# A decoder layer on one core: the first mask loaded with the weights, and a halved clock after longer stops in the account that orders TensorE

## The chip, the core and the metric

The kernel runs on one core of one Trainium2 chip. The metric is the device time of one execution in microseconds (us), as the median of several runs. A profile of one further execution shows what each engine did: TensorE (PE for its matmuls, PEld for its weight loads), VectorE (DVE), ScalarE (ACT), GpSimd (POOL) and SyncE (SP), which issues nearly all the DMA transfers.

## The reference, cut to what matters

The input x has 4 batches of 1024 rows of 256 values. One decoder layer is computed in float32, with 16 heads of 16 values each:

```python
x = x + self_attention(layernorm(x))      # causal, scores from two mixed products, biases
x = x + cross_attention(layernorm(x), ctx_1024, mask)   # 77 context rows
x = x + ffn(layernorm(x))                 # silu(x Wg') * (x Wu'), then Wd'; hidden size 768
```

In the cross attention, places where the mask is true get the score -1e9 before the softmax:

```python
scores = jnp.where(masked[:, None, :, :], NEG, scores)
```

The mask comes as 4 x 1024 x 77 booleans, one byte each. A batch's mask is 77 KB.

## The kernel before, in words

**Chunks and parts.** Each batch is cut into two chunks of 512 rows, so there are eight chunks. For each chunk the same parts are computed. `project` normalises the rows, transposes them (`L182`) and multiplies them with the key, query and value weights (`L755`, `L813`). `maxima` computes the scores once (`L853`, the causal mask added by `L861`) only to take each row's maximum on VectorE (`L866`); after every second group of heads the maxima are transposed (`L736`) and turned into a matmul operand (`L740`). `attend` computes the scores again, transposed (`L936`), subtracts the maxima with one more matmul (`L942`), takes the exponential on ScalarE (`L955`) and weighs the values (`L979`); `L668` transposes the result back and `L706` is the output product. `cross_attention` does the same against the 77 context rows (`L755` with `xwq`, maxima `L1097` and `L1105` with VectorE's `L1111`, scores `L1151`, `L1164`). `ffn` has matmuls into the hidden layer (`L1220`) and out of it (`L1254`), with ScalarE, VectorE and GpSimd in between (`L1226` to `L1231`).

**Spread tiles.** Keys and queries have to lie on other partitions than the product leaves them on. `spread` (`L713`) writes each product as two halves, hi on ScalarE (`L718`) and lo on VectorE (`L721`), and eight DMA transfers per product on SP's queue (`L727`) copy them to their places: 128 KB each, 1 MB per product.

**Start.** All weights and the rows of the first two chunks (x00, x01) are requested in the first 9 us on the queues of SP and ACT. VectorE and TensorE are ordered by hand there, until a flag "begun" is set in `maxima`; from then on TensorE alone is. The stream `late_weights` runs once "begun" is set: it builds `sel` and `selB` (`selections`, `L512` to `L524`), requests the first batch's mask (`load_mask(0)`, `L532`, its transfer is `L1015`), clears some tiles on GpSimd (`L533` to `L536`), and prepares the cross attention's weights. It ends in `load_cross(0)`, which reads the mask on VectorE: `L1038` reduces it to one value per row (`keep`), `L1040` turns it into `mneg`. `load_ffn` fetches the feed-forward weights as integers (`wi`, `L628`), GpSimd converts them (`L630`), VectorE reduces their largest value into `big` (`L632`) and TensorE transposes them (`L644`).

**What sets the order of the work.** Each part is a Python generator that yields pieces. A piece tells its TensorE time, the work that follows it on other engines, and the buffers that it takes. `weave` holds an account of the chip: the end of TensorE's last piece, the busy spans of ACT, DVE, POOL and DMA, and the time at which each buffer comes free. Again and again it computes when each stream's next piece could start, adds that stream's entry of `LATES` for the chunk, and issues the piece that could start first. So every duration in the account bears on the order of all the later pieces. There are three `pair` buffers and two `single` buffers in PSUM; a piece of `maxima` takes a `pair`, which comes free when VectorE has reduced it. TensorE executes the pieces in exactly the order written. VectorE, ScalarE, GpSimd and SP's queue also work through fixed orders of their own, so an instruction that waits there holds back what stands behind it.

The account so far let TensorE run at one speed:

```python
s.end = t + p["pe"]
if p["pe"]:
    tensor.update(end=s.end, mode=p["mode"])
```

Of the kernel before, what the change touches and what calls it, by code (L numbers as in the profile page):

```python
# [19 lines left out]
P = 128  # L20
# [7 lines left out]
def tile_decoder_layer(  # L28
# [110 lines left out]
    def x_rows(b, n):  # L139
        xt = wide([P, QT, D], "xr")  # L140
        nc.sync.dma_start(xt, x[b, n * CH : (n + 1) * CH, :].rearrange("(t p) d -> p t d", p=P))
        return xt
# [44 lines left out]
    def transpose_rows(xn):  # L187
# [2 lines left out]
        nc.scalar.copy(xnT, t)  # L190
        return xnT


    stage_cm = tc.tile_pool(name="stage", bufs=1)
    stage = stage_cm.__enter__()
# [26 lines left out]
    wo_n = rows_in(Wo, NC, F32, "wo_n", nc.sync)  # L222
    nc.sync.dma_start(bo_b, bo.partition_broadcast(P))
    x01 = x_rows(0, 1)

    et = stage.tile([P, HD, MS], F32, name="et")
    nc.vector.memset(et, 0.0)
# [200 lines left out]
        def last(self):  # L428
            return max(z for _, z in self.spans)

    tensor = {"end": 0.0, "mode": None}
    busy = {k: Engine() for k in ("ACT", "DVE", "POOL", "DMA")}
    flags = set()

# [17 lines left out]
    def piece(pe, use=(), at=0.0, cond=None, free=(), mode="whole", **take):  # L452

        return dict(pe=pe, use=use, at=at, cond=cond, free=free, mode=mode, take=take)

    def weave(*streams, until=None):
        while True:
            live = [s for s in streams if s.next is not None]  # L460
            if not live or until in flags:
                return
            can = []
            for s in live:
                p = s.next
                if p["cond"] is not None and not p["cond"]():
                    continue
                t = max(
                    tensor["end"], p["at"], *(slots[k].when(c) for k, c in p["take"].items()), 0.0
                )  # L470
                if p["pe"] and p["mode"] != tensor["mode"]:
                    t += SWITCH
                if p["use"] and p["take"]:

                    eng, us = p["use"][0]
                    t = max(t, busy[eng].start(t + p["pe"], us) - p["pe"] - 1.0)
                if t < 1.0e8:
                    can.append((t + (s.lates[s.chunk] if s.lates else 0.0), t, s))
            assert can, [s.next for s in live]
            soon = min(c[0] for c in can) + WAIT  # L480
            _, t, s = next(c for c in can if c[0] <= soon)
            p = s.next
            s.got = {k: [slots[k].take() for _ in range(c)] for k, c in p["take"].items()}
            s.end = t + p["pe"]
            if p["pe"]:
                tensor.update(end=s.end, mode=p["mode"])
            for token in p["free"]:
                give(token, s.end)
            s.done = s.end
            for eng, us in p["use"]:  # L490
                s.done = busy[eng].run(s.done + LATE, us)
            s.next = next(s.pieces, None)
# [33 lines left out]
    def late_weights(st):  # L526

        yield piece(0.0, w4=1, use=[("DVE", 4.0)], cond=lambda: "begun" in flags)
        selections(wide([P, NHP, P], "sel_f"))
        st.release("w4")  # L530
        flags.add("selections")
        load_mask(0)  # L532
        nc.gpsimd.memset(mneg, 0.0)  # L533
        nc.gpsimd.memset(xpad, 0.0)
        nc.gpsimd.tensor_copy(k2s, zero.to_broadcast(k2s.shape))
        nc.gpsimd.memset(v2, 1.0)  # L536
        nc.sync.dma_start(xwo, xWo.rearrange("(n p) f -> p n f", p=P))
        yield piece(0.0, w4=3, use=[("DMA", 4.0), ("POOL", 8.0)])
        toks = st.got["w4"]
        reorder(xwq, raw_weights(xWq))  # L540
        give(toks.pop(), st.done)
        raw = raw_weights(xWk)
        xwk = wide([P, NC, D], "xwk")
        reorder(xwk, raw)
        give(toks.pop(), st.done)
        yield piece(0.0, es=2, use=[("DMA", 4.0)])
        (t_en, t_enT) = st.got["es"]
        en = weights_tile("en").rearrange("p a b -> p (a b)")
        en = en.rearrange("p (b d) -> p b d", d=D)[:S2, :B, :]
        nc.sync.dma_start(en, enc.rearrange("b s d -> s b d"))  # L550
        enT = weights_tile("enT")[:, :, :SB]
        for c in range(NC):
            yield piece(
                0.5, single=1, use=[("DVE", 0.5)], at=st.done,
                free=[t_en] if c == NC - 1 else [],
            )
            t = single()
            for b in range(B):
                nc.tensor.transpose(
                    t[:, b * S2 : (b + 1) * S2],  # L560
                    en[:, b, c * P : (c + 1) * P],
                    ident[:S2, :S2],
                )
            nc.vector.tensor_copy(enT[:, c, :], t[:, :SB])
            st.release("single")
        yield piece(0.0, es=2)
        kk = st.got["es"]
        hi = weights_tile("khi", F32R)[:, :, :SB]
        lo = weights_tile("klo", F32R)[:, :, :SB]
        for k in range(NC):  # L570
            yield piece(
                1.1, single=1, use=[("ACT", 0.4), ("DVE", 0.5)], at=st.done + 0.5,
                free=toks if k == NC - 1 else [],
            )
            t = single()
            for c in range(NC):
                nc.tensor.matmul(
                    t[:, :SB], xwk[:, c, k * P : (k + 1) * P], enT[:, c, :],
                    start=(c == 0), stop=(c == NC - 1),
                )  # L580
            nc.scalar.copy(hi[:, k, :], t[:, :SB])
            nc.vector.tensor_tensor(
                lo[:, k, :], t[:, :SB], hi[:, k, :].bitcast(F32), ALU.subtract
            )
            st.release("single")
        nc.sync.dma_start(k2_dram[0], hi.bitcast(F32))
        nc.sync.dma_start(k2_dram[1], lo.bitcast(F32))
        for k in kk:
            give(k, st.done + 3.0)
        yield piece(0.0, w4=2, use=[("DMA", 4.0)])  # L590
        toks = st.got["w4"]
        raw = raw_weights(xWv)
        v2f = wide([P, B, D], "v2f")
        ready = st.done
        for b in range(B):
            yield piece(
                0.9, single=1, use=[("ACT", 0.4)], at=ready,
                free=[toks.pop(0), t_enT] if b == B - 1 else [],
            )
            t = single()  # L600
            for c in range(NC):
                nc.tensor.matmul(
                    t[:S2, :D], enT[:, c, b * S2 : (b + 1) * S2], raw[:, c, :],
                    start=(c == 0), stop=(c == NC - 1),
                )
            nc.scalar.copy(v2f[:S2, b, :], t[:S2, :D])
            st.release("single")
        nc.sync.dma_start(v2_dram, v2f[:S2])
        give(toks[0], st.done + 3.0)
        load_cross(0)  # L610
        flags.add("cross weights")
# [157 lines left out]
    def project(st, b, n):  # L769

        if (b, n) == (0, 0):
            yield piece(0.0, w4=1)
            xnT, t_x, at = x00T, st.got["w4"], 0.0
        else:
            yield piece(
                0.0, use=[("DMA", 4.0)] * (b > 0) + NORM, w4=1,
                cond=lambda: (("half", b - 1) if b else ("projected", 0, 0, 0)) in flags,
            )
            t_xn = st.got["w4"]
            xn = x01 if (b, n) == (0, 1) else x_rows(b, n)  # L780
            normal_rows(xn, *row_scales(xn))
            yield piece(
                1.1, use=[("ACT", 1.05)], at=st.done + LATE, pair=1, w4=1, free=t_xn
            )
            xnT = transpose_rows(xn)
            st.release("pair")
            t_x = st.got["w4"]
            at = st.done + LATE
        for c in range(NC):
# [8 lines left out]
            if c == 0:  # L798
                for i in range(QT):
                    if i % 2 == 0:  # L800
                        yield piece(
                            2.0, use=[("ACT", 1.8)] if i else [],
                            **({} if i else {"pair": 1, "v": 1}),
                        )
                        if i == 0:
# [202 lines left out]
        return nat, t_nat  # L1008


    masks, mks = {}, {}

    def load_mask(b):
        mks[b] = xpool.tile([P, NT, S2], U8, tag="mk", name="mk", bufs=2)
        nc.sync.dma_start(mks[b], mask[b].rearrange("(t p) s -> p t s", p=P))  # L1015

    def load_cross(b):

# [251 lines left out]
    def every(part, lates, chunks=range(NQ)):  # L1270
# [8 lines left out]
        return Stream(pieces, lates)  # L1279

    LATES = (
        [-0.05, 0.00, 0.00, 0.00, -0.09, 0.00, -0.11, 0.02],
        [0.00, 0.00, -0.09, 0.00, 0.00, 0.00, 0.00, -0.48],
        [0.00, 0.00, 0.00, 0.00, 0.00, 0.00, 0.00, 0.00],
        [-3.63, 0.00, 0.00, 0.00],
        [0.74, 0.00, 0.00, 0.15],
        [0.00, -0.15, -0.34, 0.00, 0.00, 0.41, 0.00, 0.00],
    )
    streams = [
        every(maxima, LATES[0]), every(cross_attention, LATES[1]), every(attend, LATES[2]),  # L1290
# [67 lines left out]
```

## Time and profile before

| what | value |
|---|---|
| median of 3 runs | 1239.33 us (1238.6 to 1239.84) |
| the profiled execution's own time | 1236.36 us |
| its span, first to last instruction | 1234.6 us |
| TensorE's matmuls busy | 1108.7 us (90% of the span) |
| VectorE busy | 729.8 us (59%) |
| ScalarE busy | 561.2 us (45%) |
| GpSimd busy | 130.5 us (11%) |
| mean granted TensorE clock | 0.956 |

The table says how busy each engine was. The granted clock is the share of its full speed that TensorE was given; at 0.5 a matmul takes about twice as long. It is recorded for every stretch of the execution, and where it is below 1, a stretch can be longer without more work in it. A row of a timeline gives the start, the duration, the engine, the line, what is written from what, and in brackets the idle time ahead of it and what ended that.

### The profile page before, as it was taken

What the parts mean: (1) busy time and instruction counts of PE and PEld (TensorE: products, weight loads), DVE (VectorE), ACT (ScalarE), POOL (GpSimd) and SP (SyncE); (2) the same over time, 40 slices, a digit from 0 to 9 for tenths busy, and PEclk for the clock granted to TensorE, in tenths of its full rate; (3) what the DMA queues carried; (4) which work ended last, traced back from release to release, by engine and by line L of the source; (5) the groups of instructions that cost most, each with busy time, mean ns of one, the idle gap of its engine ahead of it and who ended that gap; (6) DMA issues with size and microseconds to landing.
All of it is one profiled execution on the core that took longest, in us unless ns stands there. A gap on an engine that the chain in (4) does not pass through costs nothing. (4 is left out here: it accounts for less than half of the span.)

```text
span 1234.6 us, 22019 instructions
## 1 busy us (share of the span) xinstructions
PE 1108.7 (90%) x9059; PEld 683.7 (55%) x9059; DVE 729.8 (59%) x1247; ACT 561.2 (45%) x801; POOL 130.5 (11%) x138
## 2 busy tenths in 40 slices
PE   6489999999789999999899899899999899897975
PEld 4355545556556457557656456556656555456664
DVE  4577686254677867245777863652667746516443
ACT  3035455644343564653343555355344364572421
POOL 3230000001200003001200000201110000002112
PEclk9689999999999999999899899899899999998987
DMA  6973425457242014566533016363823314005000
GB/s 119 162 140 79 66 43 70 69 86 99 39 72 35 6 43 71 88 86 98 71 56 52 6 26 103 56 92 57 104 37 53 48 38 49 18 1 67 19 35 19
DMA packets 65437, 76.44 MB, mean 62 GB/s; under 512 B 22450, under 2 KB 39398, under 8 KB 65331
## 3 DMA queue, kind: packets, MB, share of 16 engines
q1 hardware_dynamic: 64227, 74.62, 38.7%
q8 instruction: 73, 1.20, 0.5%
q10 hardware_dynamic: 1104, 0.35, 0.1%
q14 instruction: 33, 0.27, 0.1%
HBM read 15.28 MB, written 9.33 MB: 20 GB/s over the span
## 5 line engine op out<-in xcount | busy, mean ns | idle before, releaser
L866 DVE TENSOR_REDUCE mt<-pair 128x2 f32<-128x1024 f32 (+3 forms) x384 | 352.6, 953 | 96.0 <-PE pair L861 60.8
L955 ACT ACTIVATE es<-pair 128x1024 f32<-128x1024 f32 (+3 forms) x384 | 300.2, 811 | 227.8 <-PE pair L949 158.1
L853 PE MATMUL pair<-k,q 64*128 64x512 f32 (+3 forms) x768 | 163.8, 432 | 39.9 <-DVE mt L866 15.1
L936 PE MATMUL pair<-q,k 64*128 64x512 f32 (+3 forms) x768 | 163.7, 423 | 18.5 <-DVE mt L866 9.7
L979 PE MATMUL single<-es,vs 128*32 128x512 f32 (+3 forms) x1536 | 163.3, 498 | 0.0
L853 PEld LDWEIGHTS pair<-k,q 64*128 64x128 f32 x768 | 76.8, 192 | 122.8 <-DVE mt L866 44.5
L942 PE MATMUL pair<-ms,sel 64*128 64x512 f32 (+3 forms) x768 | 135.8, 350 | 0.0
L936 PEld LDWEIGHTS pair<-q,k 64*128 64x128 f32 x768 | 73.5, 188 | 106.8 <-issue 38.4
L1231 POOL TENSOR_TENSOR hT<-h,hT 128x512 fp32r<-128x512 f32 x48 | 61.3, 1277 | 336.3 <-ACT hT L1230 310.4
L1153 ACT ACTIVATE es<-pair 77x1024 f32<-77x1024 f32 x64 | 63.1, 1018 | 35.6 <-PE pair L1151 35.1
L942 PEld LDWEIGHTS pair<-ms,sel 64*128 64x128 f32 x768 | 74.6, 191 | 2.8
L1254 PE MATMUL pair<-wdT,hT 128*128 128x256 f32 x384 | 61.9, 311 | 14.8 <-POOL hT L1231 4.1
L861 PE MATMUL pair<-cm_qk,id 64*128 64x64 bf16 (+1 forms) x1024 | 70.2, 214 | 0.0
L1226 ACT ACTIVATE h<-pair 128x512 f32<-128x512 f32 x48 | 28.6, 597 | 88.4 <-PE pair L1220 75.0
L949 PE MATMUL pair<-cm_kq,id 64*128 64x64 bf16 (+1 forms) x1024 | 67.0, 210 | 0.0
L1254 PEld LDWEIGHTS pair<-wdT,hT 128*128 128x128 f32 x384 | 53.8, 206 | 23.8 <-POOL hT L1231 5.2
L158 POOL TENSOR_TENSOR rs<-ve,mhalf 128x4 f32<-128x4 f32 x24 | 24.3, 1011 | 389.1 <-DVE ve L156 389.0
L1111 DVE TENSOR_REDUCE mx<-pair 128x8 f32<-128x616 f32 x64 | 48.4, 793 | 28.2 <-PE pair L1105 27.8
L1227 DVE SCALAR_TENSOR_TENSOR h<-h,pair 128x512 f32<-128x512 f32 x48 | 32.9, 684 | 54.0 <-ACT h L1226 50.0
L663 ACT COPY aS<-single 128x512 f32<-128x512 f32 x64 | 37.7, 588 | 45.5 <-PE single L1164 29.8
L190 ACT COPY xnT<-pair 128x1024 f32<-128x1024 f32 x32 | 32.5, 1014 | 48.8 <-PE pair L182 48.8
L979 PEld LDWEIGHTS single<-es,vs 128*32 128x32 f32 x1536 | 32.1, 108 | 39.7 <-issue 29.4
(180 smaller groups left out, 1589.9 us busy)
## 6 DMA issues: line engine op xcount, KB each, us to landing
q<-hi SPq DMA_DIRECT2D x128, 128.0 KB, 5.0
q<-lo SPq DMA_DIRECT2D x128, 128.0 KB, 6.0
k<-hi SPq DMA_DIRECT2D x64, 128.0 KB, 4.0
k<-lo SPq DMA_DIRECT2D x64, 128.0 KB, 6.3
xr<-in_x_dram SPq DMA_DIRECT2D x8, 512.0 KB
x<-in_x_dram SPq DMA_DIRECT2D x8, 512.0 KB, 7.1
x_dram<-x SPq DMA_DIRECT2D x8, 512.0 KB, 2.6
out_dram<-x SPq DMA_DIRECT2D x8, 512.0 KB, 3.9
```

The lines of the kernel that those rows point to most:

```text
L853: nc.tensor.matmul(t[:, j, :w], q[r, a, i * P : (i + 1) * P], k[r, a, :w], start=True, stop=True,)
L861: nc.tensor.matmul(t[:, j, w - P + 64 * half : w], id2[r, half], cm_qk[r, half, 64 * half :], start=False, stop=True, skip_group_check=True,)
L866: nc.vector.tensor_reduce(mt[:, i, :, p, kc], t[:, :, :w], AX.X, ALU.max)
L936: nc.tensor.matmul(t[:, j, lo:], k[r, a, ki * P : (ki + 1) * P], q[r, a, lo:], start=True, stop=False,)
L942: nc.tensor.matmul(t[:, j, lo:], sel[r, hp, :], ms[r, lo:], start=False, stop=True)
L949: nc.tensor.matmul(t[:, j, lo : lo + 64 * (half + 1)], id2[r, half], cm_kq[r, half, : 64 * (half + 1)], start=False, stop=True, skip_group ...
L955: nc.scalar.activation(es[:, :, lo:], t[:, :, lo:], AF.Exp)
L979: nc.tensor.matmul(acc[0][W * jj : W * (jj + 1), lo:], vs[:, ki, V1 * h : V1 * h + W], both[jj // 2][:, jj % 2, lo:], start=(kb == 0), sto ...
L1111: nc.vector.tensor_reduce(mt[:, i, h4 : h4 + 4, :].rearrange("q (k p) j -> q k (p j)", k=2), tv[:, :, :, :S2], AX.X, ALU.max,)
L1153: nc.scalar.activation(es[:S2], t[:S2], AF.Exp)
L1231: nc.gpsimd.tensor_tensor(hs[:, 1, :], h, hs[:, 0, :].bitcast(F32), ALU.subtract)
L1254: nc.tensor.matmul(t[:, i, :], h[1][:, v, i * P : (i + 1) * P], w[:, h[0], :], start=(m == 0), stop=(m == len(terms) - 1),)
```

## The change

Four edits, all in the order and the account; no matmul, reduction or transfer is added or left out.

1. `load_mask` is defined earlier, and `load_mask(0)` is called with the loads of the weights, right behind the request for x01. The call in `late_weights` goes.
2. The account keeps a time `slow`. If TensorE has stood for more than `REST` (1.3 us) ahead of a piece, `slow` is set to `COLD` (5.0 us) after the piece's start; a piece that starts before `slow` is charged with half of what is left of that stretch, at most with its own length.
3. `project` sets a flag when the second chunk's rows are normalised, and the value product of the first chunk is held back until then.
4. The entries of `LATES` have new values.

```diff
@@ beside transpose_rows @@
+    mks = {}
+
+    def load_mask(b):
+        mks[b] = xpool.tile([P, NT, S2], U8, tag="mk", name="mk", bufs=2)
+        nc.sync.dma_start(mks[b], mask[b].rearrange("(t p) s -> p t s", p=P))
@@ start @@
     x01 = x_rows(0, 1)
+    load_mask(0)
@@ the account @@
-    tensor = {"end": 0.0, "mode": None}
+    tensor = {"end": 0.0, "mode": None, "slow": 0.0}
+    REST, COLD = 1.3, 5.0
@@ weave @@
             s.end = t + p["pe"]
             if p["pe"]:
+                if t - tensor["end"] > REST:
+                    tensor["slow"] = t + COLD
+                s.end += min(max(tensor["slow"] - t, 0.0) / 2, p["pe"])
                 tensor.update(end=s.end, mode=p["mode"])
@@ late_weights @@
         flags.add("selections")
-        load_mask(0)
         nc.gpsimd.memset(mneg, 0.0)
@@ project @@
             normal_rows(xn, *row_scales(xn))
+            flags.add(("normal", b, n))
...
                             2.0, use=[("ACT", 1.8)] if i else [],
+                            cond=lambda: (b, n) != (0, 0) or ("normal", 0, 1) in flags,
                             **({} if i else {"pair": 1, "v": 1}),
@@ ahead of load_cross @@
-    masks, mks = {}, {}
-
-    def load_mask(b):
-        mks[b] = xpool.tile([P, NT, S2], U8, tag="mk", name="mk", bufs=2)
-        nc.sync.dma_start(mks[b], mask[b].rearrange("(t p) s -> p t s", p=P))
+    masks = {}
@@ LATES @@
-        [-0.05, 0.00, 0.00, 0.00, -0.09, 0.00, -0.11, 0.02],
-        [0.00, 0.00, -0.09, 0.00, 0.00, 0.00, 0.00, -0.48],
+        [0.00, 0.00, 0.00, 0.00, -0.03, 0.00, -0.31, 0.00],
+        [0.00, 0.00, 0.00, 0.00, 0.00, 0.00, -0.23, 0.00],
         [0.00, 0.00, 0.00, 0.00, 0.00, 0.00, 0.00, 0.00],
-        [-3.63, 0.00, 0.00, 0.00],
-        [0.74, 0.00, 0.00, 0.15],
-        [0.00, -0.15, -0.34, 0.00, 0.00, 0.41, 0.00, 0.00],
+        [-1.02, 0.03, 0.00, -0.48],
+        [0.54, 0.47, 0.00, 0.31],
+        [-0.20, -0.15, -0.42, -0.02, 0.00, 0.33, 0.00, 0.00],
```

The rows of `LATES` belong to, in this order: maxima, cross attention, attend, the projections of a batch's first and of its second chunk, and ffn.

## The prediction

> **What bounds the kernel now.** I read the page first, then the busy time by stretches, then the longest waits in the timeline. The page says that TensorE is the bound as a whole, and where it is not:
>
> ```profile
> PE 1108.7 (90%) x9059; PEld 683.7 (55%) x9059; DVE 729.8 (59%) x1247; ACT 561.2 (45%) x801; POOL 130.5 (11%) x138
> ...
> PE   6489999999789999999899899899999899897975
> ...
> PEclk9689999999999999999899899899899999998987
> DMA  6973425457242014566533016363823314005000
> ```
>
> The reader is to see the second and third digit: in these 62 us TensorE is half idle, the clock is lowest and the DMA engines are fullest. The stretches show how the start divides:
>
> ```profile
> core 0: us, PE busy (x) PEld busy (x) DVE busy (x) ACT busy (x) POOL busy (x), PEclk, DMA share, GB/s
> 27.40:38.30 10.90, 0.00 (x0) 0.00 (x1) 6.71 (x14) 0.69 (x1) 4.71 (x6) 0.61 1.08 123
> 38.30:50.80 12.50, 10.30 (x78) 7.88 (x78) 7.44 (x15) 1.70 (x2) 0.00 (x0) 0.66 1.07 130
> 50.80:59.40 8.60, 0.04 (x2) 0.04 (x2) 2.82 (x9) 0.00 (x0) 0.59 (x1) 0.67 1.17 213
> 59.40:92.50 33.10, 29.64 (x270) 18.04 (x270) 24.27 (x33) 10.79 (x17) 12.07 (x14) 0.83 0.78 149
> 92.50:142.80 50.30, 46.68 (x487) 27.30 (x483) 36.63 (x49) 25.79 (x53) 2.06 (x3) 1.00 0.37 72
> ```
>
> There are two stops, 10.9 and 8.6 us. The first waits for the spread keys and queries (`L727`, 126 GB/s with the DMA engines full). The second has this cause:
>
> ```profile
> 49.50 0.37 SPq L1015 DMA_DIRECT2D mk<-in_mask_BxSxS_bk_dram  x1
> 56.58 0.80 DVE L1038 TENSOR_REDUCE keep<-mk 128x8 f32<-128x616 uint8 x1 [8.51 <-DMA mk<-in_mask_BxSxS_bk_dram]
> 59.36 0.58 PE L853 MATMUL pair<-k,q 64*128 64x256 f32 x2 [8.62 <-DVE mt L866]
> ```
>
> The mask is requested behind four spread products and lands 7.1 us later. VectorE stands at `L1038`; behind it stand the reductions `L866`, so the three `pair` buffers stay full and TensorE stops. After 92.5 us TensorE is busy 46.7 of 50.3 us at full clock: from there the start's gain passes on to the end.
>
> **The change part by part.** My sum is made against the profiled execution's 1236.4 us (span 1234.6). It lies 3.0 us below the median of the runs, 1239.3, so I add 3 at the end.
>
> *The mask's load.* One request of 77 KB moves behind x01's, on SP at about 9.3 us. No spread product can be asked for before 19.57 us (the first `L727`), and from 12.5 to 20 us the DMA share is 0.06, so it lands under cover. If that cover were gone it would delay the spread keys by at most its own 7.1 us; I take 0. SP's queue now has the mask's request ahead of four spread products instead of behind them. The 8.51 us of VectorE's wait go: +8.6 us at TensorE, if nothing else is late.
>
> *The clock.* After the stop TensorE ran at half speed until about 67.3 us (the half-clock stretch of 2.5 us slices ends there), so 7.7 us of its work took twice as long: 3.9 us more. The Trainium skill, "TensorE: Matmul & The Clock Gate", section "What's actually happening", says that about 3.4 us of sustained work restore the clock; that would make it 1.7 us. The first stop speaks as the trace does (work from 39.8, full clock at about 46.9 us), so I use 3.9. Together 12.5 us are at stake.
>
> *The second chunk's normalisation comes earlier.* The order of the changed program has x01's normalisation (`L153` to `L166`) ahead of the lo half of the second key product on VectorE, and its eight transposes (`L182`, 1.97 us at 44.78) and ScalarE's copy inside the first stop instead of behind the first eight maxima. That takes 1.97 and the 1.10 us wait behind it out of the stretch 38.3 to 50.8. But TensorE then puts x01's key product (3.8 us at half clock, as `L755` at 63.36) between the seventh and eighth maxima, and VectorE has its lo half (0.75 us, behind ScalarE's 0.69) between the seventh and eighth reduction. I estimate 3 us of slip there: the eighth reduction ends near 50 instead of 46.8 us.
>
> *VectorE's chain from there.* 1.3 us of selections, 0.8 of `keep`, 2.3 of the other pieces, 6.5 of eight reductions and a lo half of 0.75 put the copy `L874` near 62 instead of 68.57 us: about 7 us earlier.
>
> *What is late next.* Before, x01's second key product was spread at 115 us. In the new order its eight transfers (1 MB, 8.3 us at 126 GB/s) stand on SP ahead of `en` and the first `wi`. The DMA engines were full from 20 to 85 us, so the feed-forward weights land later:
>
> ```profile
> 81.34 1.04 POOL L630 CAST wi<-wi 128x1024 f32<-128x1024 int32 x1 [14.14 <-DMA wi<-in_L_ffn_w_gate_dram]
> 92.00 1.21 DVE L632 TENSOR_REDUCE big<-wi 128x1 f32<-128x1024 f32 x1
> ```
>
> The cast moves from 81.34 to about 88 us (8.3, less about 1.5 for the gap at 67.5 to 70 us and the mask's place), so `big` can start near 89. VectorE comes to it after 33 reductions instead of 34, at about 83 us by the sum above (62, then 16 reductions and three small ones in 21 us). It waits some 5 to 6 us, and again reductions and `pair` buffers stand behind it. Against 92.0 that leaves 3 us. TensorE does keep more: by this place it has done x01's second key product (1.9 us, before at 110.9) and about 2 us of `attend` that came later before. I take 3 + 4 = 7, less 2 for a clock that falls in this stop: **5 us** gained at the start. Its bounds are -1 us (the whole wait and a full half-clock stretch) and 12.5.
>
> *The account and LATES.* They cost no instruction; they set another order. Up to the second batch the two orders are the same for long stretches (about 140 to 285 us), and in the second, third and last batch for others; in between feed-forward pieces lie elsewhere. For the price I use the wait for a cross attention's spread queries: it takes 14.0 us from the first `xwq` product (1122.20) to the first score:
>
> ```profile
> 1122.20 1.98 PE L755 MATMUL single<-xnT,xwq 128*128 128x512 f32 x4 [0.67 <-ACT xnT L190]
> ...
> 1136.21 1.11 PE L1105 MATMUL pair<-k2s,q 128*128 128x156 f32 x4 [4.41 <-DMA q<-hi]
> ...
> 313.04 3.69 PE L1254 MATMUL pair<-wdT,hT 128*128 128x256 f32 x16 [3.40 <-DVE mt L866]
> ...
> 779.07 1.97 PE L182 MATMUL pair<-ident,xr 128*128 128x128 f32 x8 [4.13 <-DVE xr L166]
> ```
>
> Counted in the orders with the trace's spacing (0.23 us a hidden matmul, 0.12 a `L1254`), the work inside this time falls from 13.0 to 10.0 us in the third chunk, 13.1 to 10.0 in the fifth, 9.0 to 8.1 in the last: up to 7.0 us lost. Against that, the stretches in which the stops at 313 (3.40) and 779 (4.13) lie are cut up anew: up to 7.5 us gained. I take 0 and keep -10 to +10 for the range.
>
> Does the account charge rightly? The skill's page (section "What's actually happening") lets the clock fall only after an idle window of about 3.4 us, so REST = 1.3 would charge stops that cost nothing, up to 2.5 us each. The trace has both:
>
> ```profile
> 598.40 2.68 PE L1254 MATMUL pair<-wdT,hT 128*128 128x256 f32 x16 [1.89 <-ACT es L955]
> ...
> 596.00:608.00 12.00, 9.32 (x45) 6.81 (x44) 7.22 (x13) 2.77 (x5) 2.62 (x4) 0.72 0.65 87
> ...
> 1062.00:1074.00 12.00, 9.99 (x73) 6.05 (x71) 2.12 (x5) 7.27 (x10) 0.00 (x0) 1.00 0.00 1
> ```
>
> 1.89 us at 598.40 was followed by a clock of 0.72; 2.01 us at 1064.35 by 1.00. By the page the charge would misplace pieces at the short stops (201, 598, 681, 763, 984, 1064 and 1223 us), by up to 2.5 us each; by the trace it is right about half the time. I follow the trace and give it no sign.
>
> Sum: 1236.4 - 5 + 0 = 1231.4, and 3 for the median: **1234.4 us**.
>
> **The rivals.**
> *More is kept (20%).* The wait at `big` is short, because the DMA engines catch up, or the new account also shortens later stops. For it: no wait but the mask's holds VectorE longer than 5 us in the start. Against: the full DMA engines. 12.5 us, or 5 and as much later: 1225 to 1230.
> *The wait only moves (16%).* `big` waits until 92 for `wi`, or the later order takes the gain: 1239.
> *The fill of the queries' wait is gone (24%), slower.* Feed-forward pieces are issued earlier, and the third, fifth and last chunk's cross attention lack them: 7.0 us of waits, and two new stops over 3 us, each with some 3.4 us at half clock as after 313 (1.7 us lost each): 10.4 against 5 gained, 1244.8. It decides from 7.5 us on.
> That the change does not do what it says: the mask's move stands in the program's order, so only the account could fail, as weighed above; this is within the 16%.
>
> **How the numbers follow.** My forecast has 40%. A difference of 0.2%, 2.5 us, is about what a measurement of this kernel can tell from no change. Faster: 40 + 20 = 60%; same 16%; slower 24%. The range takes in the upper case and most of the slower one: 1223 to 1247; the forecast's own range is 1230 to 1237.
>
> **What would show it.** Right: `L1038` without a wait; no stop of TensorE near 50 to 59 us; the clock at 1 from about 47 us; `L632` waiting for GpSimd's cast near 83 to 89 us; the first `nat` transpose near 138 instead of 142.8 us. Wrong: that transpose near 130 or at 143; `wi` cast before 84 us; stops over 4 us at `L1105` in the third and fifth chunk would show the slower rival.

## The result, and the profile after

The changed kernel takes 1227.74 us (median of 8 runs, 1224.94 to 1234.12) against 1239.14 us (median of 8, 1235.65 to 1240.44). The ratio is 0.9917, with a 95% interval of 0.9894 to 0.9941. So it is faster, by 11.4 us in this comparison; two more comparisons of the same kernel, told below, gave 9.3 and 7.9 us. The gain lies beyond the forecast's own range (1230 to 1237), and at the place of the rival "more is kept".

The profiled execution of after has a span of 1231.1 us and a time of 1232.86 us. That is 5.1 us above the median of its runs, while the one of before lay 2.8 us below its median. So the two profiles laid side by side show only 3.5 us of the gain, and the rest has to be looked for with care. The page first:

```profile
PE 1110.8 (90%) x9059; PEld 684.9 (56%) x9059; DVE 729.9 (59%) x1247; ACT 562.6 (46%) x801; POOL 130.8 (11%) x138
...
PE   6679989999999898999898998999999889996875
...
PEclk9798999999999999999999998999999989998986
DMA  6992315537732016555533015444826140006000
```

TensorE's instructions and their sum are those of before (1110.8 against 1108.7 us). Only the places of the stops differ: the second digit of its row rises from 4 to 6. The page's third digit of the DMA row rises too, from 7 to 9. The stretches of the start show both more finely:

```profile
core 0: us, PE busy (x) PEld busy (x) DVE busy (x) ACT busy (x) POOL busy (x), PEclk, DMA share, GB/s
27.40:38.30 10.90, 4.33 (x11) 2.24 (x11) 3.04 (x4) 1.70 (x2) 1.16 (x2) 0.69 1.08 123
38.30:50.80 12.50, 10.66 (x74) 6.74 (x74) 8.82 (x18) 1.38 (x2) 0.00 (x0) 0.73 1.08 131
50.80:59.40 8.60, 6.13 (x34) 4.10 (x34) 7.04 (x15) 0.00 (x0) 0.00 (x0) 0.60 1.08 136
59.40:92.50 33.10, 26.17 (x290) 15.42 (x292) 20.68 (x30) 14.22 (x22) 10.90 (x12) 0.96 0.98 196
92.50:142.80 50.30, 47.38 (x442) 27.36 (x441) 36.18 (x46) 23.17 (x48) 3.87 (x5) 0.93 0.20 52
```

From 50.80 to 59.40 TensorE worked 0.04 us before and 6.13 us now: the second stop is gone, though two waits of 1.70 and 1.62 us and a lowered clock (0.60) are left in its place. From 59.40 to 92.50 it does less than before (26.17 against 29.64 us), with the DMA share at 0.98 instead of 0.78. The timeline of after says what happens there. Its line numbers are shifted: `L1047` was `L1038`, `L879` was `L866`, `L738` was `L727`, `L641` and `L643` were `L630` and `L632`.

```profile
50.09 0.78 DVE L1047 TENSOR_REDUCE keep<-mk 128x8 f32<-128x616 uint8 x1
...
61.18 0.18 DVE L887 COPY mpad<-mt 128x32 f32<-128x32 f32 x1
...
74.27 3.82 SPq L738 DMA_DIRECT2D k<-hi  x4
78.19 2.47 SPq L738 DMA_DIRECT2D k<-lo  x4
81.35 0.40 SPq L639 DMA_DIRECT2D wi<-in_L_ffn_w_gate_dram  x1
...
88.31 1.04 POOL L641 CAST wi<-wi 128x1024 f32<-128x1024 int32 x1 [13.03 <-DMA wi<-in_L_ffn_w_gate_dram]
89.38 1.22 DVE L643 TENSOR_REDUCE big<-wi 128x1 f32<-128x1024 f32 x1 [4.22 <-POOL wi L641]
```

`keep` (`L1047`) no longer waits. `mpad` is copied at 61.18 instead of 68.57 us. Then the second chunk's key spread (`L738`, eight transfers) stands on SP ahead of the first `wi`, which is cast at 88.31 instead of 81.34 us, and VectorE waits 4.22 us for it. Of 8.6 us taken away, 3.55 us reach the first transpose of `nat` (a chunk's attention output): 139.24 instead of 142.79 us.

In this profile the lead then shrinks to 1.5 us at 277 us. The next gain comes after 285 us. Of before and then of after:

```profile
285.00:310.00 25.00, 22.47 (x114) 16.13 (x112) 13.03 (x28) 8.97 (x16) 3.64 (x5) 1.00 0.99 126
310.00:335.00 25.00, 19.29 (x156) 14.22 (x156) 16.18 (x24) 8.79 (x13) 5.55 (x5) 0.93 0.32 43
```

```profile
285.00:310.00 25.00, 25.00 (x132) 19.90 (x130) 15.19 (x24) 9.79 (x16) 7.69 (x6) 1.00 0.69 84
310.00:335.00 25.00, 23.11 (x262) 13.91 (x260) 18.52 (x35) 12.16 (x20) 1.21 (x2) 1.00 0.77 108
```

TensorE is busy 48.1 of these 50 us instead of 41.8: the 3.40 us stop at 313 and its lowered clock are gone, and two shorter ones at 305 and 322 (1.28 and 1.16 us) with them. The two orders can be compared exactly at the places where both have done the same matmuls. Between two such places TensorE takes 154.81 us instead of 165.12 for the same work, since it is idle for 9.0 us instead of 17.3; first before, then after:

```profile
277.12:442.24 165.12, 147.86 (x1334) 91.66 (x1334) 115.34 (x165) 70.67 (x103) 13.27 (x11) 0.99 0.34 49
```

```profile
275.66:430.47 154.81, 145.85 (x1334) 89.71 (x1333) 113.64 (x164) 70.57 (x101) 12.32 (x10) 1.00 0.43 59
```

So the lead is 11.8 us at 442 us. Later much of that is given back. New or longer stops of TensorE are

```profile
480.25 0.64 PE L1114 MATMUL pair<-k2s,q 128*128 128x156 f32 x4 [2.60 <-DMA q<-lo]
...
763.01 1.11 PE L1114 MATMUL pair<-k2s,q 128*128 128x156 f32 x4 [2.94 <-issue]
...
988.59 0.79 PE L949 MATMUL pair<-q,k 64*128 64x512 f32 x2 [3.80 <-DVE mt L879]
...
1126.23 1.11 PE L1114 MATMUL pair<-k2s,q 128*128 128x156 f32 x4 [5.33 <-DMA q<-hi]
```

With the same matmuls done, the lead is 8.4 us at the third batch's rows (500.79 instead of 509.21 us), 13.0 from 704 to 742, 10.9 at 1117, 4.8 at the last transpose of `xn` (normalised rows; 1187.03 instead of 1191.78) and 3.5 at the end. The last part, with the last chunk's cross attention and `ffn`, costs 7.4 us of it. Before, then after:

```profile
1117.42:1234.60 117.18, 87.43 (x454) 64.53 (x452) 54.46 (x97) 34.10 (x51) 23.20 (x20) 0.87 0.20 37
```

```profile
1106.48:1231.10 124.62, 88.98 (x454) 66.40 (x452) 55.91 (x97) 34.51 (x51) 23.18 (x20) 0.84 0.19 35
```

Two further profiles of after lose 7.1 and 7.2 us there. So this loss belongs to the new order and not to one execution.

### The profile page after: what moved, and what is told of

Read it like the earlier page. It is cut to its first block, busy times and chain, and to the rows that moved or that the text cites. A ratio compares the mean times of both kernels' runs of the same rounds, so it can differ in the third digit from the quotient of the medians.

```text
span 1231.1 us, 22029 instructions
## 1 busy us (share of the span) xinstructions
PE 1110.8 (90%) x9059; PEld 684.9 (56%) x9059; DVE 729.9 (59%) x1247; ACT 562.6 (46%) x801; POOL 130.8 (11%) x138
## 5 line engine op out<-in xcount | busy, mean ns | idle before, releaser
L968 ACT ACTIVATE es<-pair 128x1024 f32<-128x1024 f32 (+3 forms) x384 | 300.8, 812 | 252.6 <-PE pair L962 178.4
L879 DVE TENSOR_REDUCE mt<-pair 128x2 f32<-128x1024 f32 (+3 forms) x384 | 351.4, 952 | 92.3 <-PE pair L874 60.8
L866 PE MATMUL pair<-k,q 64*128 64x512 f32 (+3 forms) x768 | 163.2, 428 | 29.8 <-DVE mt L879 12.6
L992 PE MATMUL single<-es,vs 128*32 128x512 f32 (+3 forms) x1536 | 166.2, 506 | 0.1
L866 PEld LDWEIGHTS pair<-k,q 64*128 64x128 f32 x768 | 76.0, 188 | 121.4 <-DVE mt L879 41.7
L1114 PE MATMUL pair<-k2s,q 128*128 128x156 f32 x256 | 46.7, 308 | 12.1 <-DMA q<-hi 5.3
```

What stands on the lines that cost most here:

```text
L866: nc.tensor.matmul(t[:, j, :w], q[r, a, i * P : (i + 1) * P], k[r, a, :w], start=True, stop=True,)
L879: nc.vector.tensor_reduce(mt[:, i, :, p, kc], t[:, :, :w], AX.X, ALU.max)
L968: nc.scalar.activation(es[:, :, lo:], t[:, :, lo:], AF.Exp)
L992: nc.tensor.matmul(acc[0][W * jj : W * (jj + 1), lo:], vs[:, ki, V1 * h : V1 * h + W], both[jj // 2][:, jj % 2, lo:], start=(kb == 0), sto ...
```

## The experiments

Two theories were held against each other. A: the start gains, the new order and its account gain as much again, and the spread of the clock from run to run hides it in a single profile. B: the whole gain is the mask's; the new order is worth nothing in sum. All ratios are against before, measured on the same chip. Starts of the same work, in us of each profiled span (starts as the timeline gives them):

| kernel | first `nat` transpose | first `xn` transpose | third batch's rows | last `xn` transpose | span |
|---|---|---|---|---|---|
| before | 142.79 | 183.11 | 509.21 | 1191.78 | 1234.6 |
| after | 139.24 | 180.40 | 500.79 | 1187.03 | 1231.1 |
| after, repeated | 139.09 | 180.28 | 501.77 | 1183.91 | 1227.7 |
| mask alone | 134.57 | 174.90 | 500.84 | 1185.50 | 1227.0 |
| after, third time | 137.34 | 178.53 | 497.37 | 1183.59 | 1227.3 |
| mask alone, repeated | 134.65 | 174.94 | 502.44 | 1184.97 | 1227.1 |
| mask late | 145.18 | 186.35 | 507.96 | 1189.88 | 1232.5 |
| key spread later | 136.63 | 175.38 | 496.87 | 1182.19 | 1224.6 |
| key spread later, repeated | 142.48 | 181.22 | 502.67 | 1190.38 | 1232.0 |

**After, repeated.** The changed kernel without any edit.

> The changed kernel once more, for a second profile of it: its eight runs lie between 1224.9 and 1234.1 us, and the profiled one was among the slow ones (1232.9, clock 0.958). Theory A: the spread comes from the clock after stops, which falls in some executions and not in others at the same place; a profile of about 1226 us then shows the same stops with a clock near 0.963, and differs from the first profile where the clock was low (75 to 105 us, 760 to 1000 us). Rival: the spread comes from other waits (DMA landing times); then single stops differ by 3 us and more while the clock does not.

Measured: 1229.56 us (1224.68 to 1234.06, 6 runs) against 1238.85; ratio 0.9927 (0.9904 to 0.9950). Its profiled span is 3.4 us shorter than that of the first profile, though from 95 us on its stops are the same within 0.1 us. Most of the difference arises from 760 to 1000 us, where the first profile has 23.9 us at half clock and the repetition 13.7. Both have a stop of 1.24 us at 889 us and one of 0.97 at 892. What differs is how these stops lie in the clock's own stretches: in every trace here the clock changes only on a grid of 3.41 us, which lies elsewhere against the program's start in each execution. Three stretches of this grid, first of after, then of the repetition, with TensorE's busy time behind the length and the clock third from the end:

```profile
884.85:888.26 3.41, 3.41 (x24) 2.13 (x22) 0.68 (x2) 1.22 (x2) 1.28 (x1) 1.00 1.05 120
888.26:891.68 3.42, 1.79 (x15) 1.17 (x15) 2.88 (x5) 1.12 (x2) 1.28 (x1) 1.00 1.08 124
891.68:895.09 3.41, 2.82 (x13) 2.60 (x13) 2.07 (x4) 1.54 (x2) 1.28 (x1) 0.50 0.36 43
```

```profile
885.23:888.65 3.42, 2.65 (x20) 1.42 (x18) 0.96 (x2) 1.01 (x2) 1.28 (x1) 1.00 1.06 119
888.65:892.06 3.41, 1.98 (x18) 1.48 (x18) 2.90 (x5) 1.49 (x3) 1.27 (x1) 1.00 1.05 122
892.06:895.47 3.41, 3.38 (x28) 3.19 (x27) 1.81 (x3) 1.17 (x2) 1.28 (x1) 1.00 0.08 10
```

In after TensorE was idle for 1.63 us of one stretch, and the next two (6.8 us) ran at half clock. In the repetition the idle time was divided over two stretches (0.77 and 1.43 us), and the clock stayed full. So single profiles of this kernel differ by 3 us without a cause in its order: the first half of theory A, and the reason why the gain is read from the medians.

**The mask alone.** Before, with only the mask's load moved; TensorE's order is that of before.

```
+    mks = {}
+    def load_mask(b): ...          # moved up, as in the change
     x01 = x_rows(0, 1)
+    load_mask(0)
...
         flags.add("selections")
-        load_mask(0)
```

> The kernel before with the mask's load alone moved to the weights; TensorE's order is exactly that of before. Theory A (mask and order both count): the stop of 8.6 us at 50.8 goes, and with no second key product ahead of the feed-forward weights nothing new waits at big, so the start gains 6 to 10 us: 1229 to 1233 us, first nat transpose near 134 to 137 us, and from there the distances to before stay. Rival B (the whole gain is the mask's): 1227 to 1228 us. Rival C (the order's): 1236 to 1239 us, because the next wait takes the stop's place.

Measured: 1228.98 us (1227.0 to 1234.37, 6 runs); ratio 0.9931 (0.9912 to 0.9951), so within 1 us of the whole change beside it (1229.56). Its timeline and stretches:

```profile
46.72 0.79 DVE L1040 TENSOR_REDUCE keep<-mk 128x8 f32<-128x616 uint8 x1
...
58.17 1.18 DVE L880 COPY mpad<-mt 128x32 f32<-128x32 f32 x1
...
83.79 1.21 DVE L638 TENSOR_REDUCE big<-wi 128x1 f32<-128x1024 f32 x1
```

```profile
50.80:59.40 8.60, 7.22 (x36) 4.10 (x37) 7.37 (x10) 0.69 (x1) 2.44 (x2) 0.80 1.12 235
59.40:92.50 33.10, 28.43 (x316) 17.26 (x316) 23.61 (x33) 14.37 (x23) 10.18 (x13) 0.95 0.76 139
```

`big` comes 8.2 us earlier than before and waits for nothing, since here the first `wi` still stands ahead of the second chunk's key spread. The first `nat` transpose comes 8.2 us earlier, and 7.6 us remain at the end. The stop at 313 is still there, at 304.77 us with the same 3.40 us. So moving the mask has the whole gain by itself, as far as these medians can tell. The new order loses 4.7 us of it in the start (139.24 against 134.57; 2.7 between the later profiles of both) and regains them after 285 us.

**The mask late.** After, with the load put back.

```
     x01 = x_rows(0, 1)
-    load_mask(0)
...
         flags.add("selections")
+        load_mask(0)
```

> The changed kernel with the mask's load put back into late_weights; TensorE's order is exactly that of the changed kernel. Theory A: VectorE waits about 8 us at keep again, TensorE stops near 52 us; since the changed kernel then waits less at big (4.8 us in its profile), only 3 to 6 us of it reach the end: 1231 to 1234 us. Rival B (all is the mask's): 1238 to 1240 us. Rival C (all is the order's): 1227 to 1229 us.

Measured: 1238.56 us (1233.11 to 1245.77, 22 runs); ratio 1.0004 (0.9992 to 1.0015). The first theory was missed, and rival B came. The new order, its hold and its account together are worth nothing by themselves: the interval of the ratio leaves -1.0 to +1.9 us. The stop is longer than it was before, since the second chunk's key spread now stands ahead of the mask on SP as well (the request goes out at 56.66 us instead of 49.50):

```profile
63.79 0.79 DVE L1047 TENSOR_REDUCE keep<-mk 128x8 f32<-128x616 uint8 x1 [12.14 <-DMA mk<-in_mask_BxSxS_bk_dram]
...
65.95 0.69 PE L866 MATMUL pair<-k,q 64*128 64x384 f32 x2 [14.11 <-DVE mt L879]
```

The table shows the same balance as in after: the start loses (2.4 us at `nat`, 3.2 at `xn`), and 4.5 us come back between `xn` and the third batch (from 3.24 us later than before to 1.25 earlier). With before and "mask alone" these are all four combinations of the mask's place and the order, on one chip. Theory B holds for the sum: the mask is worth 9.0 us in the new order (1238.56 against 1229.56) and 9.9 in the old one (1238.85 against 1228.98); the new order by itself changes the time by -0.3 us with the late mask and by +0.6 with the early one, which is no difference.

**The weights on ScalarE's queue.** Is it SP's order that keeps `wi` late in after?

```
-            nc.sync.dma_start(wi, rows)
+            nc.scalar.dma_start(wi, rows)
```

> The changed kernel with the feed-forward weights requested on ACT's queue instead of SP's, so that they are not asked for behind x01's second key product. Theory A: the wait at big (first one at 89.4 us, cast at 88.3) was SP's order; the cast comes near 80 us, the wait at big goes, the first nat transpose comes 2 to 4 us earlier: 1224 to 1226 us. Rival: the DMA engines are full anyway, so the spread products land later by as much as the weights land earlier, and the time stays at 1227 to 1229 us.

Measured: 1250.45 us (1247.44 to 1251.67, 6 runs); ratio 1.0094 (1.0078 to 1.0109). Both theories were missed, on the slow side. The cast did come 13.5 us earlier than in after, but VectorE's order had changed with it:

```profile
74.78 1.04 POOL L641 CAST wi<-wi 128x1024 f32<-128x1024 int32 x1
75.85 1.22 DVE L643 TENSOR_REDUCE big<-wi 128x1 f32<-128x1024 f32 x1 [17.25 <-POOL wi L641]
...
78.48 1.11 PE L747 MATMUL single<-ident,mpad 128*128 128x128 f32 x4 [15.77 <-DVE mpad L887]
```

`big` now stands ahead of the `mpad` copy on VectorE, which waits 17.25 us at it, with TensorE behind. TensorE's order is that of after up to the third batch, yet the first `nat` transpose comes at 158.03 us, 18.8 later than in after: the whole loss is made in the start. The second and third `wi` are requested only at 108.57 and 109.06 us (83.17 and 84.39 in after), behind an exponential (`L968`) for which ScalarE had stood 3.31 us: on ScalarE's queue the requests wait for ScalarE's own work.

**The key spread later.** The same question with the requests left on SP: the second chunk's second key product is held until the first three `wi` are asked for.

```
             nc.sync.dma_start(wi, rows)
+            if part == 0:
+                flags.add(("asked", m))
...
-                st, wkT, xnT, c, bkp, (0, 1, 0, 1), 1.0, "k", at
+                st, wkT, xnT, c, bkp, (0, 1, 0, 1), 1.0, "k", at,
+                lambda: (b, n, c) != (0, 1, 1) or all(("asked", m) in flags for m in range(3)),
```

> The changed kernel with x01's second key product held back until the first three feed-forward weights have been requested; on SP its eight transfers then stand behind them, as before the change. Theory A (the new order loses 4 to 5 us in the start because VectorE waits at big for weights that land behind this product): GpSimd's first cast comes near 80 instead of 88.3 us, the wait of 4.2 us at big goes, the first nat transpose comes near 135 instead of 139.2 us, and the time is 1223 to 1226 us. Rival (the loss is the eighth reduction's wait and the smaller fill, not big): nat stays at 138 to 140 us and the time at 1227 to 1230 us.

```profile
79.76 1.04 POOL L643 CAST wi<-wi 128x1024 f32<-128x1024 int32 x1 [6.75 <-DMA wi<-in_L_ffn_w_gate_dram]
...
83.10 1.21 DVE L645 TENSOR_REDUCE big<-wi 128x1 f32<-128x1024 f32 x1
```

The cast comes 8.55 us earlier than in after, and `big` has no wait and starts 6.3 us earlier. The mechanism is shown: the eight spread transfers ahead of `wi` made the wait. In this profile the first `xn` transpose gains 5.0 us on that of after, the third batch 3.9. The time does not follow: 1230.06 us (1226.42 to 1234.79, 7 runs), ratio 0.9948 (0.9928 to 0.9968), no faster than after.

**The account and the hold, taken away one at a time.** What is the charge worth, and what the hold of the value product?

```
-    REST, COLD = 1.3, 5.0          # after without the charge
+    REST, COLD = 1.0e9, 5.0
```

> The changed kernel with REST set so high that no stop is ever charged; the values of LATES stay the new ones, so the order of the pieces is another one. Theory A (the order has no value of its own; mask alone gave the same time as the whole change): 1225 to 1235 us, with other stops at other places. Rival (the charge makes the account truer and is worth some us): 1235 us and more.

The next one is the kernel "mask alone" with the charge added, and with the old `LATES` and no hold:

```
-    tensor = {"end": 0.0, "mode": None}
+    tensor = {"end": 0.0, "mode": None, "slow": 0.0}
+    REST, COLD = 1.3, 5.0
...
+                if t - tensor["end"] > REST:
+                    tensor["slow"] = t + COLD
+                s.end += min(max(tensor["slow"] - t, 0.0) / 2, p["pe"])
```

> The kernel before with the mask's load moved and the charge in the account, the old LATES and no hold of the value product. Theory A: another order of no value of its own, 1224 to 1236 us around the 1229.0 of the mask alone. Rival (the charge is worth something without a new search of LATES): below 1225 us; or the charge alone harms: above 1236 us.

And after without the hold:

```
-                            cond=lambda: (b, n) != (0, 0) or ("normal", 0, 1) in flags,
```

> The changed kernel without the hold of the first value product. Theory A: the hold brings x01's transposes into the first stop; without it they return behind the first maxima, and TensorE's stop before the first maxima is 10 to 11 us instead of 5.6; since those 11 us end with a DMA landing either way, the first nat transpose moves by less than 2 us and the time stays within 1223 to 1234 us. Rival (the hold carries the start): 1235 us and more.

Measured, against 1238.56 us:

| kernel | us (runs) | ratio (interval) |
|---|---|---|
| after without the charge | 1310.75 (1299.48 to 1317.31, 6) | 1.0571 (1.0529 to 1.0612) |
| mask alone with the charge | 1264.01 (1257.25 to 1274.29, 6) | 1.0205 (1.0166 to 1.0245) |
| after without the hold | 1255.54 (1253.63 to 1259.01, 5) | 1.0132 (1.0111 to 1.0153) |

In all three the first theory was missed, and the rival on the slow side came, by more than it said. Without the charge VectorE comes to `big` early and waits for `wi` much longer:

```profile
73.72 1.22 DVE L643 TENSOR_REDUCE big<-wi 128x1 f32<-128x1024 f32 x1 [11.62 <-POOL wi L641]
```

Its first `nat` transpose comes at 161.75 us, 22.5 us later than in after; the other 57 are lost bit by bit later on, as by the stops of 5.54 us at 243, 4.74 at 352 and 7.69 at 644. Without the hold the first stop is back to its full length:

```profile
38.13 0.44 PE L865 MATMUL pair<-k,q 64*128 64x128 f32 x1 [10.97 <-DMA q<-lo]
```

but the first `nat` transpose even comes 1.7 us earlier than in after (137.56 us), and the loss of some 26 us is made later. The charge added to "mask alone" does the same: its `nat` comes at 138.32 us, 3.8 later than without the charge, and its span is 34.9 us longer.

So an order is not worth nothing: medians on one chip differ by up to 81 us. These three orders part from the one that they are made from nearly everywhere: at 3816 to 6103 of TensorE's 9059 matmuls another one stands in the place. "Key spread later" has a new condition and the old `LATES` as well, and cost nothing; but its order differs from that of after at 581 places only, 569 of them among the first 934 matmuls (to 147 us). So what cost 26 to 81 us (1255.54, 1264.01 and 1310.75 against about 1229.5) is for the most part not the start, but the rearranged rest. The likely reason is that the offsets in `LATES` then fall on other work; that new offsets would win the time back was not run.

**The three near ones again, on one chip.** After, "key spread later" and "mask alone", without further edits.

> The changed kernel a third time, to compare it with the next two on one chip: 1225 to 1234 us, median 1227 to 1230.

> The kernel with x01's second key product held back, a second time. Its trace was 4 to 5 us ahead of the changed kernel's from 175 us to the third batch, and its runs showed nothing of that. Theory A: the gain is real and hidden by the clock's spread from run to run; the median is 2 to 5 us below that of the changed kernel in this call. Rival: it is given back at later stops, and the two medians lie within 1.5 us.

> The mask's move alone, a second time: if the new order with its account and LATES brings nothing beyond it, the median lies within 2 us of the changed kernel's in this call; if the new order is worth what its trace gains between 285 and 500 us (4.8 us) less what it loses in the start (4.7 us), the same; if the later batches differ, 2 to 4 us above.

| kernel | us (runs) | ratio (interval) |
|---|---|---|
| after | 1229.68 (1227.41 to 1235.53, 6) | 0.9943 (0.9921 to 0.9965) |
| key spread later | 1231.88 (1228.15 to 1235.41, 11) | 0.9952 (0.9937 to 0.9966) |
| mask alone | 1231.32 (1227.31 to 1235.42, 14) | 0.9954 (0.9941 to 0.9967) |

Against 1237.62 us. The medians lie within 2.2 us, and the intervals of the ratios overlap: the three cannot be told apart. After and "mask alone" came as expected. "Key spread later" was expected 2 to 5 us below after, or within 1.5, and lies 2.2 above. Its second profile says why. The order of every engine is the same as in the first, and `big` again waits for nothing (86.36 us, the cast at 80.21). But where the first profile had the full clock, the second had 0.61 on average. The first, then the second:

```profile
66.00:92.00 26.00, 21.53 (x264) 12.53 (x264) 19.38 (x25) 12.63 (x19) 11.58 (x14) 1.00 0.73 157
```

```profile
66.00:92.00 26.00, 23.48 (x200) 12.87 (x200) 14.59 (x20) 8.55 (x12) 11.85 (x14) 0.61 0.69 148
```

With the same matmuls done, the second is as far as the first at 70 us (0.1 us apart) and 5.5 us behind when the first is at 85; its `nat` comes at 142.48 us, 5.1 later than in the third profile of after. So the lead of the first profile is no larger than what the clock alone does in these 20 us, and it did not come again. No version here beats after measurably.

## Why the prediction was right, and where not

Faster was right, and for the reason given: with the mask's load alone put back the time is that of before, and with it alone moved the time is that of after. Step by step:

- **The mask's load costs nothing: right.** `keep` waits for nothing in after or in "mask alone", and the first stop is no longer than before.
- **12.5 us at stake, of them 3.9 for the clock: too much.** "Mask alone", where nothing else moves, brings the `nat` transpose 8.2 us earlier (8.1 in its second profile), less than the stop alone. TensorE's time at half clock between 50.8 and 92.5 us, without that inside the old stop, falls only from 11.4 to 6.8 us in both profiles, so at most 2.3 us came back by the clock. What held the rest is not shown; from 50.80 to 59.40 us VectorE is busy 7.37 of the 8.60 us there. And "the clock at 1 from about 47 us" was wrong in after. Stretches of 2.5 us of its start:

```profile
48.00:50.50 2.50, 1.56 (x9) 0.49 (x7) 2.47 (x9) 0.69 (x1) 0.00 (x0) 1.00 1.10 139
50.50:53.00 2.50, 0.89 (x12) 0.59 (x12) 2.50 (x9) 0.00 (x0) 0.00 (x0) 0.80 1.06 136
53.00:55.50 2.50, 1.34 (x8) 0.75 (x8) 2.50 (x5) 0.00 (x0) 0.00 (x0) 0.50 1.11 140
55.50:58.00 2.50, 2.50 (x11) 1.87 (x10) 2.34 (x3) 0.00 (x0) 0.00 (x0) 0.50 1.09 134
58.00:60.50 2.50, 2.50 (x14) 1.70 (x13) 0.58 (x1) 0.00 (x0) 0.00 (x0) 0.84 1.05 131
```

  VectorE (third busy column) is full while TensorE waits for it in pieces of 1.70 and 1.62 us, and the clock is at half from 52.0 to 58.8 us. The stop went, and a shorter loss of clock took its place.
- **The second chunk's normalisation and VectorE's chain: right in size.** The eighth reduction ends at 48.86 us (said: near 50), `mpad` is copied at 61.18 (near 62).
- **What is late next: right.** The cast starts at 88.31 us (about 88), `big` at 89.38 (near 89) after a wait of 4.22 us (5 to 6). "Key spread later" shows the cause, by taking the eight transfers from ahead of `wi`: no wait.
- **The start gains 5 us: right.** 3.55 us at the first `nat` transpose, 3.7 and 5.5 in the other two profiles of after.
- **The account and `LATES`, "I take 0": nearly right as a sum, mis-sized in both parts.** From 144 us, where both orders have done the same matmuls, to the end of the span the lead over before changes by +0.4, +3.6 and +2.3 us in the three profiles of after. But the gain put at up to 7.5 us was 10.3 between 277 and 442 us alone, since the small stops beside 313 went as well and the clock's loss with them, and 3.3 to 5.2 more came between 570 and 704 us. Against it stand 3.0 to 4.1 us at the third chunk's queries and 7.1 to 7.4 from 1117 us on, where 7.0 had been put for all the lost fill. The waits for the third, fifth and last chunk's queries did grow (none, 1.71 and 4.41 us before; 2.60, 2.94 and 5.33 in after). That large gains and losses nearly cancel was not foreseen; the width of the range covered it.
- **"3 for the median": mis-sized.** The sum of 1231.4 us for a profiled execution lies among the three profiled times of after (1232.86, 1229.5 and 1229.06). I added 3 because the profile of before lay 3 us below its median. The profiles of after do not repeat that: they lie 5.1 above, 0.1 below and 0.6 below the medians of their runs. So some 3 us of the gain by the medians (7.9 to 11.4, where I had 5) stand between the one profile of before and the middle of its runs. Why that execution was fast is not shown.
- **"More is kept"** names the place where the time came to lie, and "the new account also shortens later stops" did happen. But it is not the cause of the gain, since "mask alone" has the gain without it, and the same order gave its later winnings back. No term of the forecast led there: that the time lies at this rival's place is in part luck. The slower rival named the right waits, but set nothing against them of what the same order wins at 305 to 322 and at 779 us.

In the sum of causes the new order itself is worth nothing. Against "mask alone", with the same matmuls done, after is 5.2 us behind at 136 us and 7.1 behind at 220, 3.1 ahead at 450 and 4.7 ahead at 1111, and behind again at the end (4.1 us by the first profiles, 0.2 by the last ones of both).

On when the clock falls, I followed the trace against the rule of an idle window of about 3.4 us, and gave the charge no sign. "Right about half the time" was a misreading: of the seven short stops named, five (598, 681, 763, 984 and 1223 us) are followed by a half clock in the trace of before, and two (201 and 1064) are not. The executions of after go further: the same stops at 889 and 892 us were followed by 6.8 us at half speed in the first profile and by none in the other two. The Trainium skill, "TensorE: Matmul & The Clock Gate", section "What's actually happening", describes windows of 3413 ns as free-running, not started by the kernel. The traces agree: the clock changes on a grid of 3.41 us. They differ from the page's rule in that a window need not be idle as a whole, for TensorE was busy 1.79 us of the window ahead of this fall. A fixed `REST` can therefore be right only on average, since the account does not know where a stop will lie in the grid. That the charge describes the clock better was not shown by any run.

Left open: how much of the spread between the comparisons (7.9 to 11.4 us) is the clock's, and whether an order that keeps its lead through the last chunk would be faster than "mask alone".

## What to carry to other kernels

When an engine that works in order stands at a small transfer, look for the request's place in its queue: moving one request of 77 KB in front of the spread transfers was the whole gain, within some 2 us. Then ask what the freed engine meets next, since here the following request (`wi`) had been pushed back by 7 us. Offsets and the account that they steer should be changed together: the new account with the old offsets lost 35 us, the new offsets without it 81. And measure the simplest part of a change alone: here it had the gain, and the rest of the change nothing.

## What was not expected of the hardware

Single executions of one unchanged program ran from 1224.7 to 1235.5 us. Stops that agree within 0.1 us were followed by a half clock in one execution and by the full clock in another (888 to 898 us), worth 3.4 us; in two executions of "key spread later" it was 5.5 us within 20.

The traces of before, after and the eleven other runs show when it falls. Cut along the grid on which the clock changes, they have 4251 windows of 3.41 us with the full clock. By TensorE's busy share in the window, the next one was at half clock so often:

| TensorE's busy share in the window | windows | followed by half clock |
|---|---|---|
| under 0.4 | 94 | 94 |
| 0.4 to 0.5 | 69 | 64 |
| 0.5 to 0.6 | 63 | 40 |
| 0.6 to 0.7 | 106 | 12 |
| 0.7 to 0.9 | 821 | 7 |
| 0.9 and more | 3098 | 0 |

So in these runs it is the busy share of a window that counts, with the turn near one half, and not the length of a single stop. One stop of 1.7 us can fill half of a window or a quarter of two, as chance has it. The busy times are the profile's, in which the ends of matmuls are modelled, so the edge may be sharper than it looks. The clock rows of one profile can therefore not be used to price a stop to better than some 3 us.
